# A graph layer on one Trainium2 core: where the two parts of x begin in SBUF

## The chip, the cores and the metric

The kernel runs on one core of a Trainium2 chip. The metric is device time in microseconds (us). Before the change the median of three runs is 1513.1 us (1511.35 to 1513.92). TensorE (PE) does the matmuls and, as a separate stream, their weight loads (PEld); VectorE is DVE, ScalarE is ACT, GpSimd is POOL, and SyncE (SP) issues most of the DMAs.

## The reference

A message-passing layer with 6,250 nodes of 64 features and 200,000 edges, sorted by their target `dst`:

```python
w = silu(edge_attr @ W1 + b1) @ W2 + b2            # 9 weights per edge
h_src = features[src]                              # a row of x per edge
msg = einsum('ef,em,fmg->eg', h_src, edge_sh * w, W_tp)
agg = segment_sum(msg, dst, num_segments=N) / sqrt(E / N)
emb = silu(c_noise[:, None] @ Wn1 + bn1) @ Wn2 + bn2
gamma, beta = split(emb, 2, axis=-1)
x = layernorm(x + agg * (1 + gamma) + beta)
```

`E` in the square root is the constant 100000 of the reference, so the root is 4. `gamma` and `beta` come from one number per node.

## The kernel before, in words

**Tiling.** The edges lie in 1,563 tiles of 128, one edge per partition. 16 tiles make a group; there are 98 groups (`NBLK`). The main loop takes one group per turn, and the order of work is written out by hand: an instruction runs on its engine in the order in which the program names it.

**Getting x[src], in three ways.** Each of the 16 tiles of a group needs 128 rows of x in the tile `hs`.

- *Gathers* (`gather`, L97 to L102): an indirect DMA of POOL per tile, issued `AHEAD` = 6 groups ahead; 1,173 of them in all, 11 to 13 in a group.
- *Picks* (`pick`, L488 to L511): 3 or 4 tiles of a group (`picked`) are fetched by TensorE. All of x is kept in SBUF, node number = p * 49 + h * 7 + l with p the partition, h and l from 0 to 6. x is split into two parts, `xs[0]` (x rounded to the matmul's fp32r type, a cast of ACT in L245) and `xs[1]` (what the rounding left, a subtraction of DVE in L246); each is a tile of 128 partitions x (7 h, 64 features, 7 l) floats, 12,544 bytes per partition. For each h, DVE makes a one-hot block of 128 partitions x 128 edges (`hot_k`, L485, seven buffers of 7 blocks, 512 bytes a block). A pick is 14 matmuls (L500): for each h and each part, the one-hot block is loaded as weights and the slice `xs[i][:, h]` of 64 x 7 = 448 columns, 1,792 bytes, is streamed through. They add up in one PSUM tile `px`. Then DVE keeps the right one of 7 l (L509, with a mask from `li` and `jl`) and sums over l (L511) into `hs`.
- *Rows by SP* (`load_rows`, L107 to L115): every fourth group has one tile whose rows are copied by single DMAs.

**The rest of a group.** `hidden` (L428) and `second` (L445) are the small network on the edge attributes, `weights` (L455 transposes, L461 and L467) makes the tile `a`, `windows` (L533) multiplies the rows `hs` with `a` for each tile, `project` (L579) applies W_tp, `turn` (L585) transposes the tile `rt` that it gave, `place` (L595) adds the sums to their nodes with another one-hot `c` and `bring` and `finish_nodes` end the nodes. The first matmul of `windows` waits for the group's gathers. In one turn i the program names the picks of group i + 1, `windows(i)`, and every other turn `project`; `windows(i)` stands behind pick 0 of group i + 1 and ahead of its other picks. Small pieces of `weights`, `nodes` and `turn` are put between the matmuls of a pick (`other`).

**Where tiles begin.** Tiles of a pool lie one behind the other in each partition. `even` (L61) rounds small tiles up to 32 floats, 128 bytes. By the sizes in the code, `xs0`, `xs1` and every `hot_k` buffer begin at a multiple of 128 bytes, and so do all slices of x (1,792 = 14 x 128) and all one-hot blocks.

**Setup.** The first pick begins while x is still being split: the matmuls follow the slices `xs[i][:, h]` one by one.

Of the kernel before, what the change touches and what calls it, by code (L numbers as in the profile page):

```python
# [11 lines left out]
F32R = mybir.dt.float32r  # L12
# [4 lines left out]
P = 128  # L17
N, F, M, D, H, E = 6250, 64, 9, 32, 64, 200000
NJ = 49
# [11 lines left out]
J = 7  # L31
# [29 lines left out]
def even(pool, p, n, dt, **kw):  # L61

    per = 32
    return pool.tile([p, -(-n // per) * per], dt, **kw)[:, 0:n]
# [3 lines left out]
def gnn_resnorm_kernel(ctx: ExitStack, tc: tile.TileContext, x, src, dst, dst_row, ea, sh, cn,  # L68
# [18 lines left out]
    with ExitStack() as fast:  # L87
# [3 lines left out]
        keep = fast.enter_context(tc.tile_pool(name="keep", bufs=1))  # L91
# [26 lines left out]
        ident2 = keep.tile([P, F], F32)  # L118
        w2p = keep.tile([P, D], F32)
        b2c = even(keep, P, 1, F32, name="b2c")  # L120
        xs = [keep.tile([P, J, F, J], F32R, name=f"xs{i}") for i in range(2)]
        wi = even(keep, P, W, F32, name="wi")
        nf = keep.tile([P, 2 * P], F32)
        lo = even(keep, P, NBLK, F32, name="lo")
# [785 lines left out]
```

## Time and profile before

| | us |
|---|---|
| median of 3 runs | 1513.1 |
| the profiled execution | 1512.09 |
| its span, first to last instruction | 1510.2 |
| PE busy | 1459.4 (97%) |
| weight loads busy | 1207.7 (80%) |
| DVE busy | 1152.7 (76%) |
| POOL busy | 1113.2 (74%) |
| ACT busy | 514.6 (34%) |

The mean granted TensorE clock is 0.989. It is 1.00 from 49.6 us to 1493.5 us after the start and partly 0.50 outside of that.

How to read the views: the page gives busy time of each engine and the costliest groups of instructions, each with its line, its engine, "output<-inputs", shapes, count, busy time, mean ns of one, and the idle time just before it. Matmuls overlap in their pipeline, so the mean ns of one is its latency; how fast they follow each other has to be read from starts, or from the chain of waits, which lists pieces with start, time and count. The chain of waits follows the work that ended last back to the beginning.

### The profile page before, as it was taken

What the parts mean: (1) busy time and instruction counts of PE and PEld (TensorE: products, weight loads), DVE (VectorE), ACT (ScalarE), POOL (GpSimd) and SP (SyncE); (2) the same over time, 40 slices, a digit from 0 to 9 for tenths busy, and PEclk for the clock granted to TensorE, in tenths of its full rate; (3) what the DMA queues carried; (4) which work ended last, traced back from release to release, by engine and by line L of the source; (5) the groups of instructions that cost most, each with busy time, mean ns of one, the idle gap of its engine ahead of it and who ended that gap; (6) DMA issues with size and microseconds to landing.
All of it is one profiled execution on the core that took longest, in us unless ns stands there. A gap on an engine that the chain in (4) does not pass through costs nothing.

```text
span 1510.2 us, 34381 instructions
## 1 busy us (share of the span) xinstructions
PE 1459.4 (97%) x10984; PEld 1207.7 (80%) x10984; DVE 1152.7 (76%) x2044; ACT 514.6 (34%) x1326; POOL 1113.2 (74%) x1182
## 2 busy tenths in 40 slices
PE   5899999999999999999999999999999999999996
PEld 3688788878787888787878888788888888888885
DVE  6777877777868777778687788777886877877774
ACT  3333333333423333334233333243342333333342
POOL 7777777777777777777777777777777777777770
PEclk9899999999999999999999999999999999999997
DMA  5422222222222222222222222222222222222210
GB/s 166 97 72 64 72 58 64 55 59 70 65 57 73 58 64 54 69 61 65 54 73 54 60 54 73 60 55 54 71 62 54 72 55 60 70 58 60 72 30 7
DMA packets 90424, 96.30 MB, mean 64 GB/s; under 512 B 36824, under 2 KB 51370, under 8 KB 90234
## 3 DMA queue, kind: packets, MB, share of 16 engines
q1 hardware_dynamic: 52122, 53.89, 12.0%
q0 software_dynamic: 37536, 38.51, 11.6%
q8 instruction: 90, 1.47, 0.4%
q10 hardware_dynamic: 576, 1.61, 0.3%
q14 instruction: 100, 0.82, 0.2%
HBM read 92.17 MB, written 1.73 MB: 62 GB/s over the span
## 4 chain that ended last, share of the span: by engine, by line
PE 84%; DVE 6%; ACT 2%; issue 2%; SPq 2%; POOL 2%; DMA 1%; DVEq 0%; POOLq 0%; ACTq 0%
PE px L500 63%; PE pz L533 6%; PE p L428 5%; PE p L445 3%; PE pt L579 3%; POOL hs L99 2%; SPq L115 1%; PE p L455 1%; ACT L436 1%; DMA hs<-in_x_dram,src_i 1%; ACT st L436 1%; DVE xm L509 1%; PE ps L595 1%; DVE hs L511 1%; PE ps L625 1%
## 5 line engine op out<-in xcount | busy, mean ns | idle before, releaser
L99 POOL DMA_INDIRECT hs<-in_x_dram,src_i x1173 | 1111.9, 948 | 359.5 <-issue 316.9
L500 PE MATMUL px<-xs,hot_k 128*128 128x448 f32 x5138 | 1136.1, 374 | 2.0 <-ACT xs L245 1.3
L500 PEld LDWEIGHTS px<-xs,hot_k 128*128 128x128 f32 x5138 | 929.7, 189 | 93.5 <-DVE xs L246 3.2
L509 DVE SCALAR_TENSOR_TENSOR xm<-li,jl,px 128x448 f32<-128x448 f32 x367 | 248.3, 677 | 231.7 <-PE px L500 231.7
L485 DVE TENSOR_TENSOR hot_k<-pk,nk 128x896 fp32r<-128x896 f32 x367 | 382.7, 1081 | 1.9 <-PE pk L231 1.9
L436 ACT ACTIVATE st<-p,b1c 128x1024 f32<-128x1024 f32 x98 | 109.1, 1114 | 399.6 <-PE p L428 399.3
L511 DVE TENSOR_REDUCE hs<-xm 128x64 f32<-128x448 f32 x367 | 227.6, 620 | 12.6
L543 ACT COPY ztw<-pz 64x140 f32<-64x140 f32 (+1 forms) x780 | 208.6, 267 | 16.5 <-PE pz L533 5.3
L533 PEld LDWEIGHTS pz<-a,hs 128*64 128x64 f32 x3116 | 100.0, 138 | 43.5 <-issue 42.7
L467 DVE TENSOR_TENSOR a<-oh,p 128x1008 f32<-128x1008 f32 x98 | 118.0, 1204 | 3.3
L533 PE MATMUL pz<-a,hs 128*64 128x63 f32 x3116 | 113.4, 225 | 3.0 <-issue 2.0
L428 PE MATMUL p<-ea,w1bd 64*128 64x512 f32 x392 | 111.6, 646 | 0.0
L601 ACT COPY carry<-ps 128x128 f32<-128x128 f32 x48 | 12.8, 266 | 277.2 <-PE ps L595 277.2
L461 DVE TENSOR_TENSOR p<-p,sh 128x72 f32<-128x72 f32 x196 | 47.0, 240 | 59.1 <-PE p L455 27.4
L445 PEld LDWEIGHTS p<-st,w2p 128*32 128x32 f32 x784 | 15.8, 108 | 89.3 <-issue 43.9
L728 ACT ACTIVATE var<-var,eps 128x2 f32<-128x2 f32 (+1 forms) x25 | 7.4, 295 | 207.5 <-DVE var L725 207.5
L445 PE MATMUL p<-st,w2p 128*32 128x256 f32 x784 | 63.1, 393 | 15.4 <-DVE xb L369 7.9
L579 PE MATMUL pt<-ztw,wtc 128*64 128x112 f32 x960 | 55.3, 261 | 2.7 <-ACT st L436 2.5
L479 ACT CAST pk<-kr 128x512 f32<-128x512 f16 (+1 forms) x96 | 54.2, 564 | 1.7 <-DMA kr<-kd 1.7
L455 PE MATMUL p<-ident,p2s 128*128 128x128 f32 x196 | 53.5, 273 | 0.1
L428 PEld LDWEIGHTS p<-ea,w1bd 64*128 64x128 f32 x392 | 29.7, 186 | 29.8 <-issue 26.4
L579 PEld LDWEIGHTS pt<-ztw,wtc 128*64 128x64 f32 x960 | 46.8, 137 | 4.6 <-ACT st L436 4.0
(139 smaller groups left out, 528.5 us busy)
## 6 DMA issues: line engine op xcount, KB each, us to landing
hs<-in_x_dram SPq DMA_DIRECT2D x2944, 0.2 KB
ea<-in_ea_dram SPq DMA_DIRECT2D x48, 512.0 KB
hs<-in_x_dram,src_i POOLq DMA_INDIRECT x1173
kr<-kd SPq DMA_DIRECT2D x48, 256.0 KB
sh<-in_sh_dram SPq DMA_DIRECT2D x49, 144.0 KB
cb<-cn_d SPq DMA_DIRECT2D x12, 128.0 KB
out_dram<-o SPq DMA_DIRECT2D x24, 64.0 KB
dst_i<-in_dst_dram SPq DMA_DIRECT2D x1, 768.0 KB
```

The costliest lines, as they stand in the source:

```text
L99: hs_dma[g] = [nc.gpsimd.indirect_dma_start(out=hs[g][:, t - g * KB, :], out_offset=None, in_=x, in_offset=bass.IndirectOffsetOnAxis(ap=sr ...
L428: nc.tensor.matmul(p1[:, i, :], w1bd[i * 64:(i + 1) * 64, :], e[i * 64:(i + 1) * 64, :], start=True, stop=True)
L436: nc.scalar.activation(st[g], p1_t.pop(g), AF.Silu, bias=b1c)
L445: nc.tensor.matmul(p2[g][c * D:(c + 1) * D, 0, :].rearrange("p (i e) -> p i e", i=2), w2p, s[:, :, c * P:(c + 1) * P], start=True, stop=True)
L467: nc.vector.tensor_mul(a[g], oh_t.pop(g)[:, :, None, :].to_broadcast([P, KB, M, W]), sw.unsqueeze(3).to_broadcast([P, KB, M, W]))
L485: nc.vector.tensor_tensor(hot_k[g, t], pk_t[g][:, t, None, :].to_broadcast([P, J, P]), nk.unsqueeze(2).to_broadcast([P, J, P]), op=ALU.is_ ...
L500: nc.tensor.matmul(px.rearrange("p f l -> p (f l)"), hot_k[g, t][:, h, :], xs[i][:, h].rearrange("p f l -> p (f l)"), start=(h == 0 and i ...
L509: nc.vector.scalar_tensor_tensor(xm, li[:, None, :].to_broadcast([P, F, J]), jl[:, c:c + 1], px, op0=ALU.is_equal, op1=ALU.mult)
L511: nc.vector.tensor_reduce(hs[g][:, tiles(g) - q + t, :], xm, AX.X, ALU.add)
L533: mm = nc.tensor.matmul(pz[v][v * F:(v + 1) * F, k // 2].rearrange("p m w -> p (m w)"), hsg[:, k0 + k, :], ag[:, k0 + k].rearrange("p m w ...
L543: nc.scalar.copy(z[h * F:(h + 1) * F, 0:5 - h, k0 + v:k0 + n:2, :].rearrange("p m k w -> p k m w"), pz[v][v * F:(v + 1) * F, 0:(n + 1 - v) ...
L579: nc.tensor.matmul(pt[h * F:(h + 1) * F, 0, 0:KW], wtc2[:, c, :], z[h][:, c], start=(c == 0), stop=(c == 4))
```

## The change

Both parts of x move into one tile `xs_w` with 12,544 + 128 bytes for each part. Within its 12,672 bytes (99 x 128) each part begins 8 floats, 32 bytes, behind the start. So all slices of both parts begin 32 bytes behind a multiple of 128. The tile is 256 bytes larger than the two before together, so everything that lies behind it moves by 256 bytes, the one-hots among it. No instruction is named, added or left out; the slices have the same shapes.

```diff
-        xs = [keep.tile([P, J, F, J], F32R, name=f"xs{i}") for i in range(2)]
+        xs_w = keep.tile([P, 2, NJ * F + 32], F32R)
+        xs = [xs_w[:, i, 8:8 + NJ * F].rearrange("p (h f l) -> p h f l", h=J, f=F) for i in range(2)]
```

## Prediction

> **What bounds the kernel now.** I read the page's busy shares first, then the chain that ended last, then the costliest groups.
>
> ```profile
> span 1510.2 us, 34381 instructions
> ...
> PE 1459.4 (97%) x10984; PEld 1207.7 (80%) x10984; DVE 1152.7 (76%) x2044; ACT 514.6 (34%) x1326; POOL 1113.2 (74%) x1182
> ...
> PE px L500 63%; PE pz L533 6%; PE p L428 5%; PE p L445 3%; PE pt L579 3%; POOL hs L99 2%; SPq L115 1%; PE p L455 1%; ACT L436 1%; DMA hs<-in_x_dram,src_i 1%; ACT st L436 1%; DVE xm L509 1%; PE ps L595 1%; DVE hs L511 1%; PE ps L625 1%
> ...
> L99 POOL DMA_INDIRECT hs<-in_x_dram,src_i x1173 | 1111.9, 948 | 359.5 <-issue 316.9
> L500 PE MATMUL px<-xs,hot_k 128*128 128x448 f32 x5138 | 1136.1, 374 | 2.0 <-ACT xs L245 1.3
> L500 PEld LDWEIGHTS px<-xs,hot_k 128*128 128x128 f32 x5138 | 929.7, 189 | 93.5 <-DVE xs L246 3.2
> ```
>
> TensorE is busy 97% of the span, and 63% of the last chain is the line that the change touches: 5,138 matmuls that stream a slice of x (448 columns) against a one-hot block (128 columns of weights). They wait for almost nothing (2.0 us). The mean of 374 ns is latency; the rate is in the chain of waits, in stretches where only these matmuls stand:
>
> ```profile
> 45.33 4.82 PE px L500 x13
> ...
> 775.78 8.10 PE px L500 x40
> 834.84 10.53 PE px L500 x52
> ```
>
> The later two give 8.10/40 = 10.53/52 = 202.5 ns for one. The first was at half clock. Its time by stretch:
>
> ```profile
> 45.40:49.40 4.00, 4.00 (x11) 3.58 (x12) 0.50 0.46 108
> 1440.60:1447.20 6.60, 6.60 (x34) 5.96 (x32) 1.00 0.12 28
> ```
>
> The column behind the brackets is the granted clock, 0.50 and 1.00. The trace's single starts at 0.50 lie 373 to 374 ns apart. If a matmul were only its columns, full clock would make that 373.5/2 = 186.8 ns. It is 202.5, so 15.7 ns of each matmul don't scale with the array's clock. The other matmul of this type (fp32r, L595, 256 columns) takes about 119 ns to the next start, against 186.8 x 256/448 = 106.7: 12.4 ns too many. A lack of columns per second would grow with the columns and leave 9.0 there; it looks rather like a nearly fixed loss per matmul and weight load. The weight load of matmul k+1 begins 2 to 4 ns after matmul k, so two streams read SBUF side by side, and today both begin at multiples of 128 bytes. The trace can't tell me more: no L500 pair has another offset.
>
> **The second bound** is POOL. 74% busy hides it: each gather has 0.94 us busy and 0.30 us of its own issue.
>
> ```profile
> 1469.86 0.94 POOL L99 DMA_INDIRECT hs<-in_x_dram,src_i  x1 [0.30 <-issue]
> 1471.11 0.94 POOL L99 DMA_INDIRECT hs<-in_x_dram,src_i  x1 [0.30 <-issue]
> 1472.36 0.94 POOL L99 DMA_INDIRECT hs<-in_x_dram,src_i  x1 [0.30 <-issue]
> ```
>
> One gather every 1.25 us, 1,173 of them, from 4.0 to 1472.4 us: 1173 x 1.25 = 1466 us with no real wait for TensorE. A group's windows (L533) start 27 to 29 us after its last gather issued as far as group 60, and 17 to 21 us after it for the last five groups. That lead is all that a faster TensorE can eat.
>
> **The change, part by part.**
>
> 1. Instructions. None is added, removed or moved; no queue is passed. The tile grows by 256 bytes per partition, 2 x 128, so all tiles behind it, the one-hots too, keep their place modulo 128. Cost 0.
>
> 2. Setup. xs is written by 7 casts (L245, median 0.96 us) and 7 subtractions (L246, median 0.94 us); 32 bytes are 8 elements, and the shapes stay. The slices of one h remain disjoint, so the first pick should still follow the slices one by one from 9.0 us. If one tile were instead waited for as a whole, the pick would start behind the last subtraction (15.9 us). Its 14 matmuls take at most 14 x 0.37 = 5.2 us, so it would end near 21 us and not 16.6: a loss of up to 4.5 us, at the least 0. I take 0, since each part's slices shared a tile before too.
>
> 3. The stream. What 32 bytes do to the 202.5 ns is shown nowhere. Bounds: the most that can go is the whole excess, 15.7 ns, 5138 x 15.7 = 81 us of TensorE. On the other side the nearest row is L585, whose weights (rt) lie at 0 and at 64 behind a multiple of 128 in turn: the L500 start before it to its own start is 203.2 and 205.8 ns on the mean of 24 and 23. 2.6 ns on each L500 matmul would be 5138 x 2.6 = +13 us. The far bound is a second stall as large as the first, +15.7 ns, +81 us. All of a loss counts, since TensorE sets the end. Of a gain only part counts (below). I take the gain: the half-clock row says that the excess is memory time and not array time, and a start offset between two streams is what can alter that.
>
> [...]
>
> **Where a gain ends.** A group has 3.75 picks of 14 matmuls on the mean, so full relief saves 52.5 x 15.7 = 0.82 us a group, and the lead of 28 us is gone after some 35 groups. From there TensorE waits at L533 for gathers at POOL's 15 us a group. The end, backwards: group 94's last gather issued at 1434.6, and its packets end 1.1 us later, so its windows can start at 1435.7 (now 1451.6). To the windows of 95 it is now 14.9 us with 4 picks in it, less 56 x 15.7 ns = 0.9: 1449.7. To those of 96, 18.7 us with 5 picks, less 1.1: 1467.3. From there to the end is now 1510.2 - 1485.2 = 25.0 us with one pick, less 0.2: 1492.1. The last gather has landed by 1474.4, before it is wanted. So the span falls by 18.1 us and not by 81. About 1 us more goes to waits that are new at L533: -17 us. The profiled execution took 1512.1 us for its span of 1510.2; 17 less is 1495, and from the median 1513.1 it is 1496. Relief of 17/5.138 = 3.3 ns a matmul is enough for most of it; less relief pays 5.1 us per ns. Own range 1492 to 1504.
>
> **Rivals.**
>
> - *Nothing (the excess has nothing to do with low address bits).* For it: L500 takes the same 202.5 ns for all 7 one-hot buffers and all 14 slices of x. Against: all of these are multiples of 128 apart. Time 1513. A change that doesn't do what it says (a tile base that isn't a multiple of 128) ends here too; the sizes in the code speak against it.
> - *Slower: an odd start costs each moving read.* [...] It decides from 0.6 ns per matmul (0.6 x 5138 = 3 us, 0.2%), because TensorE has no slack for 97% of the span. Price: at the L585 row's 2.6 ns 1526; at a doubled excess 1594. For it: the excess shows that this stream has no reserve at full clock. Against: the windows (L533) read their moving operand at every multiple of 4 bytes modulo 128 and start 51 to 52 ns apart at nearly all of them, but they are plain fp32 and run at a lower rate.
> - *Setup waits as a whole.* +4.5 us, 1518, if nothing else changes.
>
> **How the numbers follow.** Relief with POOL as the floor: 0.48, 1496. Nothing: 0.12. Slower by the odd start: 0.38, of which 0.13 lies above 1558. Slower by the setup alone: 0.02. A measurement here can tell about 0.2% (3 us) from no change. So faster 0.48, same 0.12, slower 0.40. The range reaches from 1492 (relief's own low end) to 1558, leaving out 0.04 below and 0.13 above; it holds cases of both signs, so the likeliest one's range, 1492 to 1504, is what I'd act on.
>
> **What would show it.** In the profile after, L500 alone in the chain should give about 187 to 192 ns for one in the stretches before group 30, the weight load to weight load distance the same, L533 should gain waits that end on the gathers or their landing, and TensorE's busy share should fall to some 93% while POOL's rises above 74%. Gathers must stay 1.25 us apart. If L500 stands at 202.5, the rival "nothing" is right; if above it, the odd start costs. If L500 falls and the span doesn't, another engine than POOL took over: DVE, at 76%, is the next.

## The result and the profile after

The change is slower: 1519.39 us median of 5 runs (1517.38 to 1519.98) against 1511.35 us before (five runs, the three of above among them, 1510.41 to 1513.92), a ratio of 1.0044 (95% interval 1.0033 to 1.0056). The profiled execution took 1519.98 us, its span is 1518.2 us. Ten of the experiments below ran on chips on which every kernel, the one before too, took 2,400 to 2,570 us; from those only starts in stretches of one granted clock are used, never times.

The page after: instructions are the same in number, only PE's busy time is up (1467.2 against 1459.4 us). Lines are one higher than before, since the diff adds a line.

```profile
span 1518.2 us, 34381 instructions
...
PE 1467.2 (97%) x10984; PEld 1208.8 (80%) x10984; DVE 1152.2 (76%) x2044; ACT 514.2 (34%) x1326; POOL 1113.1 (73%) x1182
...
PE px L501 60%; PE pz L534 6%; POOL hs L99 5%; PE p L429 5%; PE pt L580 3%; PE p L446 3%; DMA hs<-in_x_dram,src_i 2%; PE p L456 1%; ACT L437 1%; DVE xm L510 1%; ACT st L437 1%; DVE hs L512 1%; PE ps L596 1%; PE ps L626 1%; DMA gam<-in_x_dram 0%
...
L99 POOL DMA_INDIRECT hs<-in_x_dram,src_i x1173 | 1111.8, 948 | 359.5 <-issue 314.2
L501 PE MATMUL px<-xs_w,hot_k 128*128 128x448 f32 x5138 | 1142.1, 374 | 2.6 <-ACT xs_w L246 1.3
```

The mean of 374 ns hasn't moved. It is latency, and a reader who looks only at it sees nothing. The chain that ended last, in order of time (start, us, what, count), shows the rate:

```profile
778.93 8.14 PE px L501 x40
838.14 10.59 PE px L501 x52
```

8.14/40 = 203.5 and 10.59/52 = 203.7 ns for one, against 202.5 before: about 1.1 ns. POOL's gathers stay 1.25 us apart, and the last is issued when it was before, so the gathers neither gained nor lost:

```profile
1471.08 0.94 POOL L99 DMA_INDIRECT hs<-in_x_dram,src_i  x1 [0.31 <-issue]
1472.33 0.94 POOL L99 DMA_INDIRECT hs<-in_x_dram,src_i  x1 [0.30 <-issue]
```

The single starts say which matmuls pay. From a matmul on the first part of x to the next start it is 204.5 ns (202.6 before), from one on the second part 202.7 (202.4). Within the tile the parts lie 12,672 = 49.5 x 256 bytes apart. So the first begins 32 bytes behind a multiple of 256 and the second 160 behind one, while both began at a multiple of 256 before. Here and below a "start to start" is the mean over matmuls of this line with one of their kind before and two behind them, at granted clock 1.00 and without gaps over 260 ns, some 2,900 to 3,800 of a run. The rest of the 5,138 stand beside another kind of matmul or at half clock.

**Where the 8.0 us of the span come from.** The starts of the same matmul in both executions can be compared one by one. Outside of the setup and of one stretch of half clock the change falls behind by 4.4 us over 5,000 matmuls of this line, or 0.9 ns each. Some 2.7 us more come from that stretch of half clock, 955.0 to 961.8 us, which the profiled execution of before hadn't: TensorE (L446) waits 2.9 us there for n_bad, which DVE makes in L353, and in this execution the clock fell. PE after:

```profile
955.84 1.08 PE L446 MATMUL p<-st,w2p 128*32 128x256 f32 x8 [2.93 <-DVE n_bad L353]
956.85 1.98 PE L534 MATMUL pz<-a,hs 128*64 128x63 f32 x32
958.76 1.12 PE L501 MATMUL px<-xs_w,hot_k 128*128 128x448 f32 x2
...
960.70 1.57 PE L501 MATMUL px<-xs_w,hot_k 128*128 128x448 f32 x4
```

and the same place before:

```profile
952.18 0.64 PE L445 MATMUL p<-st,w2p 128*32 128x256 f32 x8 [2.94 <-DVE n_bad L352]
952.75 1.15 PE L533 MATMUL pz<-a,hs 128*64 128x63 f32 x32
953.83 0.67 PE L500 MATMUL px<-xs,hot_k 128*128 128x448 f32 x2
...
954.88 2.47 PE L500 MATMUL px<-xs,hot_k 128*128 128x448 f32 x11
```

From the small network's matmul to the last pick shown it is 4.86 us after and 2.70 before; the rest of the 2.7 us falls to the picks up to 961.8. The last 1.0 us lies in the setup, where the half-clock stretches fall elsewhere (16.3 to 23.1 us instead of 25.8 to 32.6).

### The profile page after: what moved, and what is told of

Same layout as the page of the kernel before. It is cut to its first block, busy times and chain, and to the rows that moved or that the text cites. A ratio compares the mean times of both kernels' runs of the same rounds, so it can differ in the third digit from the quotient of the medians.

```text
span 1518.2 us, 34381 instructions
## 1 busy us (share of the span) xinstructions
PE 1467.2 (97%) x10984; PEld 1208.8 (80%) x10984; DVE 1152.2 (76%) x2044; ACT 514.2 (34%) x1326; POOL 1113.1 (73%) x1182
## 4 chain that ended last, share of the span: by engine, by line
PE 80%; DVE 6%; POOL 5%; DMA 3%; issue 3%; ACT 3%; DVEq 0%; SPq 0%; POOLq 0%; ACTq 0%
PE px L501 60%; PE pz L534 6%; POOL hs L99 5%; PE p L429 5%; PE pt L580 3%; PE p L446 3%; DMA hs<-in_x_dram,src_i 2%; PE p L456 1%; ACT L437 1%; DVE xm L510 1%; ACT st L437 1%; DVE hs L512 1%; PE ps L596 1%; PE ps L626 1%; DMA gam<-in_x_dram 0%
## 5 line engine op out<-in xcount | busy, mean ns | idle before, releaser
L501 PE MATMUL px<-xs_w,hot_k 128*128 128x448 f32 x5138 | 1142.1, 374 | 2.6 <-ACT xs_w L246 1.3
L501 PEld LDWEIGHTS px<-xs_w,hot_k 128*128 128x128 f32 x5138 | 929.1, 189 | 99.8 <-DVE xs_w L247 3.4
L446 PEld LDWEIGHTS p<-st,w2p 128*32 128x32 f32 x784 | 15.8, 108 | 89.2 <-issue 43.9
L446 PE MATMUL p<-st,w2p 128*32 128x256 f32 x784 | 63.2, 394 | 15.3 <-DVE xb L370 7.8
L449 ACT ACTIVATE p2s<-p,b2c 128x256 f32<-128x256 f32 x98 | 45.7, 466 | 16.3 <-PE p L446 16.3
```

The lines of the kernel that those rows point to most:

```text
L446: nc.tensor.matmul(p2[g][c * D:(c + 1) * D, 0, :].rearrange("p (i e) -> p i e", i=2), w2p, s[:, :, c * P:(c + 1) * P], start=True, stop=True)
L501: nc.tensor.matmul(px.rearrange("p f l -> p (f l)"), hot_k[g, t][:, h, :], xs[i][:, h].rearrange("p f l -> p (f l)"), start=(h == 0 and i ...
```

## The experiments

Eighteen kernels ran.

**1. Is it the merged tile, the place, or the part?**

```diff
 e1_merged_only
-        xs_w = keep.tile([P, 2, NJ * F + 32], F32R)
-        xs = [xs_w[:, i, 8:8 + NJ * F]...
+        xs_w = keep.tile([P, 2, NJ * F + 0], F32R)
+        xs = [xs_w[:, i, 0:0 + NJ * F]...
 e2_both_32_of_256
+        xs_w = keep.tile([P, 2, NJ * F + 64], F32R)
+        xs = [xs_w[:, i, 8:8 + NJ * F]...
 e3_both_160_of_256
+        xs_w = keep.tile([P, 2, NJ * F + 64], F32R)
+        xs = [xs_w[:, i, 40:40 + NJ * F]...
 e4_one_hots_shifted_too
+                hot_k[g, t] = late.tile([P, J * P + 32], F32R, ...)[:, 8:8 + J * P].rearrange("p (h e) -> p h e", h=J)
```

> Both parts in one tile, but without the 32 bytes: 12,544 bytes each, so both begin at multiples of 256 as before. Theory A (the start address costs): 202.6 ns from matmul to matmul in L501 and a time within 0.15% of before, 1511 to 1513 us. Theory B (one tile instead of two costs, by waits on the whole tile): the time of the change, about 1518 us, and later first picks.

Measured: 1511.86 us, ratio 1.0001 (0.9992 to 1.0010), 202.5 ns. Theory B falls: the single tile costs nothing.

> As the change, but with 12,800 bytes for each part, so both parts begin 32 bytes behind a multiple of 256 (in the change the second begins 160 behind one). Theory A1 (the place modulo 256 decides: 32 costs 2.2 ns, 160 costs nothing): both matmuls of a pair take about 204.8 ns to the next start; 5138 x 2.2 = 11 us of TensorE and a time of about 1523 us. Theory A2 (the role decides: only the first part's matmul is lengthened, whatever lies in the second): 204.8 and 202.5 ns as in the change and about 1518 us.

Measured: 1528.58 us, ratio 1.0111 (1.0096 to 1.0126); 205.9 and 205.8 ns for the two parts. A2 falls, and the place modulo 256 decides as in A1, but the step is larger than the 2.2 ns that the mixed kernel showed.

> Both parts begin 160 bytes behind a multiple of 256. Theory A1 (modulo 256): 202.5 ns for both matmuls and about 1512 us, although each part still begins 32 bytes behind a multiple of 128. Theory A2 (the role): 204.8 and 202.5 ns and about 1518 us.

Measured: 1505.40 us, ratio 0.9951 (0.9938 to 0.9965), 200.5 ns for both parts. This is *faster than before*, with both parts 32 bytes behind a multiple of 128, as the change names them. Neither theory had that. Chains of e1, e2 and e3:

```profile
834.58 10.53 PE px L501 x52
```

```profile
1084.58 10.74 PE px L501 x52
```

```profile
1009.99 10.41 PE px L501 x52
```

Divided by 52: 202.5, 206.5 and 200.2 ns (long stretches lie up to 0.6 ns off the mean over all starts). In the change the two parts mix a slow place and a fast one: (205.9 + 200.5)/2 = 203.2, measured 203.5.

> The change, and the one-hots moved by 32 bytes too (each buffer grows by 128 bytes, so buffers begin 32 or 160 behind a multiple of 256 in turn). Theory A3 (the distance of the two streams decides): with both moved alike the 2.2 ns go away, wholly or in the buffers that have the same place as the slice, and the time falls towards 1512 us. Theory A4 (the stream's own start decides, whatever the weights do): 204.8 and 202.5 ns in all buffers and about 1518 us.

Measured: 1517.77 us, ratio 1.0037 (1.0023 to 1.0051); 203.6 to 203.9 ns in each of the four pairings of places. The time is what A4 said and the pattern isn't: the parts no longer differ. Parts and buffers both alternate here. By the distances found below the pairs would take 202.5 and 203.7 ns, 203.1 on the mean, and it is some 0.6 above that mean: where places alternate, as here and in the change, a matmul's own pair doesn't give its rate.

**2. A sweep of the place of x**, the one-hots at a multiple of 256. The diff is e2's with 16, 32, 48, 56 and 24 floats in place of 8.

> Both parts begin 64 bytes behind a multiple of 256. So far one L501 matmul takes 202.5 ns at 0, 205.9 at 32 and 200.5 at 160 behind a multiple of 256. Theory W (a slope over the 256 bytes, 5.3 ns down per 128 bytes, with a jump at the multiple of 256): 204.5 ns, about 1522 us. Theory S (two separate causes: 32 behind a multiple of 64 costs 3.4 ns, the upper half of the 256 bytes gains 5.3): 202.5 ns, 1512 us.

Measured: 1505.91 us, ratio 0.9957 (0.9941 to 0.9974), 200.2 ns.

> Both parts begin 128 bytes behind a multiple of 256. Theory W (slope): 201.9 ns, about 1510 us. Theory S (two causes): 202.5 - 5.3 = 197.2 ns; that is 27 us of TensorE, of which POOL lets some 17 through: about 1496 us.

Measured: 1516.91 us, ratio 1.0029 (1.0016 to 1.0041), 203.7 ns.

> Both parts begin 192 bytes behind a multiple of 256. Theory W (slope): 199.2 ns, about 1499 us, where POOL's gathers begin to hold TensorE up. Theory S (two causes): 197.2 ns, about 1496 us.

Measured: 1513.60 us, ratio 1.0005 (0.9996 to 1.0015), 202.2 ns.

> Both parts begin 224 bytes behind a multiple of 256, which is again 32 behind a multiple of 64. Theory W (slope): 197.9 ns, the lowest of the row, about 1496 us. Theory S (two causes): 200.5 ns as at 160, about 1505 us.

Measured: 1517.27 us, ratio 1.0033 (1.0022 to 1.0043), 203.7 ns.

> Slices 96 bytes behind a multiple of 256, one-hots at one. Measured: 0 gives 202.5, 32 205.9, 64 200.2, 128 203.7, 160 200.5, 192 202.2, 224 203.7 ns. If the pattern repeats after 96 bytes (32 and 128 slow, 64 and 160 fast, 0 and 96 and 192 between), 96 gives 202.3 ns and about 1512 us. If 64 to 96 is one fast stretch, 200 ns and 1505 us.

Measured: 205.4 ns (no time); neither guess.

Both W and S fall: the row has no slope and no two additive parts. The fastest, s64, has these stretches in its chain:

```profile
1010.92 10.41 PE px L501 x52
1069.19 10.41 PE px L501 x52
```

**3. The place of x, or its distance to the one-hots?** A tile of 32, 224 or 192 bytes is put ahead of the one-hots, and one behind them that makes it up to 256, so nothing else changes its place modulo 256. x lies in one tile as in e2, at 0 or 32. (L504 below is L500 with the added lines.)

```diff
+        keep.tile([P, 8], F32, name="ahead")              # 56: 224 bytes, 48: 192
...
+                if (g, t) == (0, 0):
+                    late.tile([P, 56], F32, tag="behind", name="behind", bufs=1)
```

> Slices of x and one-hot blocks all begin 32 bytes behind a multiple of 256. Theory R (only the distance between the two streams counts): as at 0 and 0, 202.5 ns for one L501-type matmul and about 1512 us. Theory M (only the place of the streamed slice counts): as at 32 and 0, 205.9 ns and about 1528 us. Anything else: both places count.

> Slices at a multiple of 256, one-hot blocks 224 behind one, so that the distance is 32 as in the run with both parts at 32. Theory R (distance): 205.9 ns and about 1528 us. Theory M (place of the slice): 202.5 ns and about 1512 us.

Measured: 202.8 ns with both at 32, 205.8 ns with x unmoved and the one-hots at 224.

> Slices and one-hot blocks both 32 bytes behind a multiple of 256: distance 0. Theory R (the distance of slice and block modulo 256 decides): 202.5 ns per L501-type matmul and the time of before, about 1512 us. Theory M (the place of the slice alone decides): 205.9 ns and about 1528 us.

> Slices at a multiple of 256, one-hot blocks 224 behind one: distance 32. Theory R: 205.9 ns and about 1528 us although x has not moved. Theory M: 202.5 ns and about 1512 us.

> Slices at a multiple of 256, one-hot blocks 192 behind one: distance 64. Theory R: as with the slices moved by 64, 200.2 ns and about 1506 us. Theory M: 202.5 ns and about 1512 us.

Measured: 202.6, 205.8 and 200.3 ns. Chains of d0_both_32_again, w2_x0_hot224 and d64_x0_hot192, each followed by the line of the windows for the same stretch (the granted clock is the column behind the brackets):

```profile
1791.55 10.55 PE px L504 x52
```

```profile
1791.60:1802.00 10.40, 10.40 (x52) 9.39 (x50) 1.00 0.11 26
```

```profile
1654.14 7.84 PE px L504 x38
```

```profile
1654.20:1661.90 7.70, 7.70 (x38) 6.75 (x36) 1.00 0.12 26
```

```profile
1746.20 10.41 PE px L504 x52
```

```profile
1746.30:1756.50 10.20, 10.20 (x52) 9.32 (x50) 1.00 0.12 26
```

202.9, 206.3 and 200.2 ns. Theory M falls, and R holds at the three distances tried: moving the weights alone gives the same rate as moving x alone by the same distance. Start to start by the distance of slice to block, modulo 256 bytes:

```
distance   x moved      one-hots moved
   0       202.5        202.6, 202.8 (both moved by 32)
  32       205.9        205.8, 205.8, 205.9
  64       200.2        200.3, 200.3
  96       205.4
 128       203.7
 160       200.5
 192       202.2
 224       203.7
```

The distance counts modulo 256 and not modulo more: within a run it alternates modulo 512 and 1,024, since slices lie 7 x 256 bytes apart, and the means of these classes differ by at most 0.3 ns (205.7 to 206.0 in e2). DVE writes the one-hots, so these writes lie at the same distance from x as the weight loads. They aren't the cause: between starts during which no DVE instruction ran, 870 to 940 in a run, it is 202.7 ns at distance 0 (before), 206.5 at 32 (e2), 200.2 at 64 (s64) and 200.2 at 160 (e3).

> x at a multiple of 256, one-hots 224 behind one: distance 32. Theory R: 205.8 ns a matmul and, as when x was moved by 32, about 1528 us. Theory M (place of x alone): 202.5 ns and about 1512 us.

> x at a multiple of 256, one-hots 192 behind one: distance 64. Theory R: 200.2 ns a matmul and, as when x was moved by 64, about 1506 us. Theory M: 202.5 ns and about 1512 us.

Measured: 205.9 and 200.3 ns. The times came out at 0.989 and 1.000 of before, but the runs of before beside them spread by 3.7% (2,402.7 to 2,491.2 us), so they don't settle a step of 1%. With x moved R is shown in rate and time, with the one-hots moved in rate alone.

**4. Does the excess over 186.8 ns belong to the weight load?**

```diff
-                    nc.tensor.matmul(px.rearrange("p f l -> p (f l)"), hot_k[g, t][:, h, :],
+                    nc.tensor.matmul(px[0:F].rearrange("p f l -> p (f l)"), hot_k[g, t][:, h, 0:F],
...
+            nc.scalar.copy(hs[g][F:P, tiles(g) - q + t, :], ident[F:P, 0:F])
```

> Each pick loads only the first 64 of the 128 columns of a one-hot block as weights, so half of the edges of a pick get no row of x (their rows are filled with a constant by ACT); slices at a multiple of 256. A matmul still streams 448 columns, 186.8 ns by the half-clock row. Theory L (the excess comes from the weight load that runs beside the stream, and grows with its columns): the excess of 15.7 ns halves, about 194.5 ns. Theory O (the excess is the stream's own start, whatever is loaded): 202.5 ns.

> The same with half of the weight columns, slices 32 bytes behind a multiple of 256. Theory L: the 3.4 ns that this place costs with full weights shrink with the load, to about 1.7 ns over the other run with half weights. Theory O: 205.9 ns, 3.4 over it.

Measured: 202.5 ns at distance 0, as with full weights. That is O's number, and L falls; O's reason, the stream's own start, falls too, by section 3. At distance 32 neither number comes: of the 149 picks whose matmuls follow one another without a break, 42 run at 200.0 ns and the rest at about 206.5, and the mean over all starts is 204.4. The h32 chain, and the windows of the same stretch, in the slower of the two:

```profile
472.25 8.26 PE px L501 x40
```

```profile
472.30:480.40 8.10, 8.10 (x40) 5.13 (x38) 1.00 0.11 25
```

8.26/40 = 206.5 ns. Half as many columns to load let a pick take one of two rates at this distance, and don't shrink the loss in proportion. What sets which of the two stays open.

At half clock the distance does nothing. A whole pick of 14 matmuls takes the same time at distance 32 (w2_x0_hot224) and at 64 (d64_hot192_time), each line followed by its line of the windows:

```profile
2251.19 5.60 PE L504 MATMUL px<-xs_w,hot_k 128*128 128x448 f32 x14 [4.84 <-issue]
```

```profile
2251.20:2256.70 5.50, 5.50 (x14) 4.46 (x14) 0.50 0.03 6
```

```profile
2308.55 5.60 PE L504 MATMUL px<-xs_w,hot_k 128*128 128x448 f32 x14 [6.37 <-issue]
```

```profile
2308.60:2314.10 5.50, 5.50 (x14) 4.42 (x14) 0.50 0.18 45
```

Over the 310 to 370 starts at half clock in each such run it is 373.3 ns at distances 0, 32, 64 and 96 alike. So what the distance costs or gains is no fixed amount per matmul; it appears only at full clock. How large the excess is at distance 0 rests on taking the half-clock row for the bare columns, which no run tests.

## Why the prediction was wrong, point by point

- **The bound** was right: TensorE's rate in this one line set the time, and nearly every ns in it counted. In e2 the starts in the middle of the program fall behind by 14.5 us, 2.9 ns for each matmul of the line, where 3.4 ns x 5138 would be 17. That the medians lie 1528.58 - 1512.19 = 16.4 us apart, close to 17, is partly luck: about 1.0 us of it comes from the setup and 1.4 from a half-clock stretch in the profiled execution.
- **Instructions** (0) were right, and **setup** (0) was for the merged tile, as e1 shows: the first pick follows the slices one by one, and the casts keep their 0.96 us. With x at another place the setup was about 1 us longer all the same: in all eight such profiled executions of 1,500 to 1,530 us the matmuls of L232 at 19.1 to 19.3 us take 2.07 to 2.08 us, in before and e1 1.16, and the second pick starts 0.7 to 0.9 us later. In the change they lie in the half-clock stretch of 16.3 to 23.1 us; why the clock fell earlier there stays open.
- **The stream** is the step that failed, in sign and in size: it took 15.7 ns off each matmul, and the change put 1.0 ns on. "I take the gain" rested on two thoughts. The first read the excess as time that doesn't scale with the clock and as nearly fixed per matmul. The half-clock row doesn't say so: the prediction halved it as bare columns, with no excess in it, but an excess that doesn't scale would stand in it too. What the distance changes, at least, isn't of that kind, since 373.3 ns stand at 0, 32, 64 and 96 alike. That the excess is memory time was argued and is not shown. The second, that an offset between the streams removes it, does not hold: over eight distances the rate moves between 200.2 and 205.9 ns, so at best 2.3 ns of the 15.7 go and at worst 3.4 come. At least 13 of the 15.7 ns remain at every distance, and also with half of the weights; what they are stays open.
- **"32 bytes behind a multiple of 128"** was taken as one place. It is two, 32 and 160 behind a multiple of 256, one slow and one fast. All L500 pairs of the trace before were multiples of 256 apart, so it could not show this; the table of sizes could: 12,544 is 49 x 256, 12,672 is not a multiple.
- **The row for the loss**, L585 with its 2.6 ns, gave a fair size for the wrong reason. By the sizes in the code the two rt tiles begin 128 and 64 behind a multiple of 256, distances of 128 and 192 to the slices of then; for those the sweep gives 203.7 and 202.2 ns, the opposite order.
- **The weights' side.** The measured rate changes from 202.5 to 205.8 or 200.3 ns when only the weights are moved (distances 32 and 64), so at full clock their place does bear on the running matmuls here.
- **POOL as the floor of a gain** never came into play. In s64 the windows of the last five groups still start 12 to 16 us behind their last gather. Its gain of 6.2 us is smaller than 2.3 x 5138 = 12: its profiled execution has a half-clock stretch at the same wait (948.3 to 951.7 us, 1.5 us) and a setup that ends 1 us later, and between these the starts gain 7.7 us, 1.5 ns for each matmul. (The lead itself was read short: as far as group 60 it is 27 to 33 us before, not 27 to 29.)
- **The rival that happened** is "slower: an odd start costs each moving read", in place, sign and deciding size (1 ns against 0.6). That an odd start of the moving read costs by itself isn't what the runs show: 160 is as odd as 32 and is fast (200.5 ns against 205.9), and moving only the weights does the same (205.8). (The windows' 51 to 52 ns, in the row against it, are one step of two: the trace of before has 3,116 records for 1,563 tiles, and from every second start to the next it is 58 to 59 ns, 2,716 times of 2,928. So 63 columns of a tile take about 58 ns there, 1.1 a ns, against 448 in 202.5 ns, 2.2 a ns.) The range of 1492 to 1558 held 1519 because it covered both signs; no row of the trace before led to this size.

Why the distance matters isn't settled: the row 202.5, 205.9, 200.2, 205.4, 203.7, 200.5, 202.2, 203.7 has no order that these runs explain. That 16-byte steps or other matmul lengths would follow it wasn't tried.

## What to carry to other kernels

Where an fp32r matmul and the next weight load run side by side at full clock (here the load began 2 to 4 ns after the matmul) and TensorE sets the time, the distance of their start addresses modulo 256 bytes is worth a sweep: here 64 and 160 bytes made a whole kernel 0.4 to 0.5% faster than before and 32 made it 1.1% slower, for one changed number. Look at the rate in the chain of waits, not at the mean duration, which stood at 374 ns before and after, and work out every address modulo more than the alignment that you have in mind. An unexplained excess in a rate is no gain until a run has moved it.

## What else the runs showed

The granted clock fell to 0.50 at a single wait of 2.9 to 3.0 us in the middle of the program (L446 behind n_bad) in six of the ten profiled executions of 1,500 to 1,530 us (at 955.0 us in the change, 948.3 in s64) and not in the other four, before and e1 among them, which waited as long. A stretch of 6.8 us (the change, s128, s192) cost 2.5 to 2.7 us, one of 3.4 us (e2, e3, s64) some 1.5.
